# One product in sixteen of a selective scan, on VectorE or on GpSimd

## The chip, the cores and the metric

The kernel runs on one core of a Trainium2 chip. The metric is the device time of one execution in microseconds; each kernel's figure is the median of its timed runs. One further execution is profiled, and its trace gives the durations.

## The reference

Four layers follow each other on an image batch of 4 x 64 x 64 x 128. Layers 0 and 1 are selective state-space scans over the image in four directions (rows, columns, and both backwards), with 128 channels in layer 0 and 256 in layer 1, and 16 states per channel. Layer 2 is a gated message passing over 3 x 3 neighbours, layer 3 a neighbourhood attention. The change lies in the scans of layers 0 and 1. In layer 1's form (layer 0 does the same):

```python
delta = jax.nn.softplus(dts + dt_b[None, :, :, None])
A = -jnp.exp(A_log).reshape(K, DI, N)

def step(h, t):
    x_t, d_t, B_t, C_t = t
    h = jnp.exp(d_t[..., None] * A) * h + (d_t * x_t)[..., None] * B_t[:, :, None, :]
    return (h, jnp.einsum('bkdn,bkn->bkd', h, C_t))
```

For every position, the term that is added to the state is (delta * x) * B, where B belongs to one of 16 states and is the same for all channels; the state times C is summed over the 16 states.

## The kernel before, in words

**Units, steps, tasks.** A task is one image and one block of 128 channels: 4 tasks in layer 0, 8 in layer 1. A task has 16 steps: four directions, each cut into four chunks of 1024 positions (`TS`). There are 192 steps. A step has 16 units (`NG`), numbered here 0 to 15: a unit is 8 channels times 16 states on the 128 partitions, by 1024 positions. Two successive units form a pair, and a pair shares one `h` tile of 128 x 2048.

**The way of a unit.** SP, the queue of SyncE, loads delta * x of 8 channels into the unit's half of the `h` tile, repeated for the 16 states (`load`, line 451), ten units ahead (`LEAD`). TensorE spreads delta into PSUM (`decay`, line 465, tile `da`, two buffers), and ScalarE makes exp(delta * A) of it in place (line 467). VectorE multiplies the pair by B (`times`, line 457), and then runs one `tensor_tensor_scan` for each unit (`scan`, line 476), in place in `h`. ScalarE copies the last states (`save`, line 494), and GpSimd multiplies the pair by C (`times`, line 457 again). TensorE adds up over the states into the bank `yps` (`add_up`, line 557), four units later (`LAG`). After that the `h` tile, one of nine, is free for a new load.

**B and C.** B is repeated over the 8 channels by TensorE into PSUM (`bring_b`, line 502, tile `B`). C is repeated by a transfer: `repeat`, lines 382 to 385, reads each of the 16 rows of C from DRAM eight times into the SBUF tile `repC`, 512 KB.

**Preparation and side work.** For each step, `prepare` computes delta and delta * x 28 units ahead (`AHEAD`), on TensorE, ScalarE and GpSimd (tiles `xd`, `delta`, `low`, `parts`), stores delta * x to DRAM (`dud`), and moves delta's three bf16 parts into place with twelve transfers (line 426). Between the units, a planner sets in "side" work: projections, depthwise convolutions (they load `pad` tiles), convolutions and what comes after the scans, for the images before and behind. Such operations are issued through line 102.

**Order.** The order of every engine is fixed when the program is built; nothing is reordered on the chip. The loop `run` goes over the units and writes scan, products, decay and sums in that order. The class `Plan` keeps an estimated clock, 3.6 us a unit, and an estimated time for TensorE, ScalarE and GpSimd; `slot` adds the cost of a unit's own work, and side work is set in where its estimated start fits. Transfers are posted with a due time and issued by SP in order. Each transfer also waits until the one eight places before it has landed. `fill` adds matmuls with zero weights (line 562) where TensorE has little to do.

Of the kernel before, what the change touches and what calls it, by code (L numbers as in the profile page):

```python
# [10 lines left out]
BF16 = mybir.dt.bfloat16  # L11
# [6 lines left out]
P = 128  # L18
# [3 lines left out]
T = 512  # L22
NCH = L // T
ROWS = T // HW
NS = 16
ND = 4
NG = 16
TS = 1024
# [16 lines left out]
class Consts:  # L45


    def __init__(self, tc, pool, d_gather, d_spread):
        nc = tc.nc

        gather = pool.tile([P, 56], F32, name="gather")
        nc.sync.dma_start(out=gather, in_=d_gather)
        self.gather = [gather[:, 24 - 8 * jj : 56 - 8 * jj] for jj in range(4)]

        self.spread = pool.tile([P, 4, P], BF16, name="spread")
        with tc.tile_pool(name="spread32", bufs=1) as tmp:
            spread = tmp.tile([P, 4, P], F32, name="spread32")
            nc.sync.dma_start(out=spread, in_=d_spread)
            nc.vector.tensor_copy(self.spread, spread)
        self.nothing = pool.tile([P, P], BF16, name="nothing")  # L60
        nc.vector.memset(self.nothing, 0.0)
        self.ones16 = pool.tile([P, T], BF16, name="ones16")
        nc.vector.memset(self.ones16, 1.0)
        self.ident = pool.tile([P, P], F32, name="ident")
        make_identity(nc, self.ident)
        self.ones128 = pool.tile([P, P], F32, name="ones128")
        nc.vector.memset(self.ones128, 1.0 / 128.0)
        self.cen128 = pool.tile([P, P], F32, name="cen128")
        nc.vector.tensor_sub(self.cen128, self.ident, self.ones128)
        self.cen256 = pool.tile([P, P], F32, name="cen256")  # L70
        self.neg256 = pool.tile([P, P], F32, name="neg256")
        nc.vector.memset(self.neg256, -1.0 / 256.0)
        nc.vector.tensor_add(self.cen256, self.ident, self.neg256)
        self.eps = pool.tile([P, 1], F32, name="eps")
        nc.vector.memset(self.eps, EPS)
# [35 lines left out]
UNIT = 3.6  # L111
# [7 lines left out]
class Plan:  # L119
# [22 lines left out]
    def post(self, chain, issue, due=0.0):  # L142

        if self.running:
            self.posted.append((chain, max(self.done, due), issue))
        else:
            issue()
# [11 lines left out]
    def slot(self, u, sums, copies):  # L159
        at = self.at  # L160
        self.now = u * UNIT
        self.flush()
        at["PE"] = max(at["PE"], self.now) + 1.1
        at["ACT"] = max(at["ACT"], at["PE"]) + 1.1
        if u % 2 == 0:
            at["POOL"] = max(at["POOL"], self.now) + 4.5
        at["PE"] += sums
        at["ACT"] += copies

# [111 lines left out]
AHEAD = 28  # L281
LEAD = 10
LAG = 4


class Scans:
# [52 lines left out]
    def prepare(self, t, step):  # L339

        nc, W, half, post = self.plan, t.W, self.half, self.plan.post
        begin = self.plan.now
        k, c = t.steps[step]
        R = W.rank
        rows = R + 2 * NS
        if t.first is None:
            yield "PE" if W.nct > 1 else "PE ACT"

        xd = self.xds[step % 2]
        if t.first is None:  # L350
            xdd = t.xdd[step] = self.dram.tile(
                [rows, TS], F32, name="xdd", tag=f"xdd{W.layer}", bufs=(4, 2 * len(t.steps))[W.layer]
            )
            ps = self.bank()
            for ti in range(W.nct):
                for i in range(HALVES):
                    nc.tensor.matmul(
                        image(ps[i * H : (i + 1) * H, :]),
                        W.xp[:, ti, k, :],
                        self.view(t.xc[ti], k, c, i, HALVES),  # L360
                        start=ti == 0,
                        stop=ti == W.nct - 1,
                    )
                if ti + 1 < W.nct:
                    yield "PE ACT" if ti + 2 == W.nct else "PE"
            nc.scalar.copy(xd, ps)

            def store_xd():
                for i in range(HALVES):
                    nc.sync.dma_start(out=xdd[:, half(i)], in_=xd[i * H : i * H + rows, :])  # L370

            post("prep", store_xd)
            ready = max(self.plan.done, self.plan.now) + LANDING
            yield "PE ACT"
        else:
            xdd, ready = t.first.xdd[step], begin
            for i in range(HALVES):
                nc.sync.dma_start(out=xd[i * H : i * H + rows, :], in_=xdd[:, half(i)])
            yield "PE ACT", self.plan.now + LANDING
        out = t.prepared[step] = {"xd": xd}  # L380

        def repeat():
            out["C"] = self.tile("repC", 2)
            src = bass.AP(xdd.tensor, xdd.offset + (R + NS) * TS, [[TS, NS], [0, 8], [1, TS]])
            nc.sync.dma_start(out=out["C"], in_=src)

        post("rep", repeat, max(begin + 15 * UNIT, ready))

        bias = W.dtb[:, k, t.ct : t.ct + 1]
        delta, low = self.tile("delta", 1), self.tile("low", 1)  # L390
        for i in range(HALVES):
            ps = self.bank()
            nc.tensor.matmul(
                ps,
                W.dtw[i * H : (i + 1) * H, k, t.ct * P : (t.ct + 1) * P],
                xd[i * H : (i + 1) * H, :],
                start=True,
                stop=True,
            )
            nc.scalar.activation(low[:, half(i)], ps, AF.Abs, bias=bias)  # L400
            nc.scalar.activation(delta[:, half(i)], ps, AF.Relu, bias=bias)
            yield "PE ACT" if i + 1 < HALVES else "ACT"
        nc.scalar.activation(low, low, AF.Exp, scale=-1.0)
        yield "ACT"
        nc.scalar.activation(low, low, AF.Ln, bias=1.0)
        yield "POOL"
        nc.gpsimd.tensor_add(delta, delta, low)
        yield "ACT POOL"
        parts = self.tile("parts", 1, shape=(P, 3, TS), dtype=BF16)
        nc.scalar.copy(parts[:, 0, :], delta)  # L410
        nc.gpsimd.tensor_mul(image(low), image(delta), self.view(t.xc[t.ct], k, c, 0, 1))
        yield "POOL"
        t.x_done = step == len(t.steps) - 1
        dud = out["du"] = self.dram.tile([P, TS], F32, name="dud", tag="dud", bufs=3)
        post("prep", lambda: nc.sync.dma_start(out=dud, in_=low))
        nc.gpsimd.tensor_sub(delta, delta, parts[:, 0, :])
        yield "ACT"
        nc.scalar.copy(parts[:, 1, :], delta)
        yield "POOL"
        nc.gpsimd.tensor_sub(parts[:, 2, :], delta, parts[:, 1, :])  # L420


        def own(part, j):
            if j == part == 0:
                out["delta"] = self.dps[step % 2]
            nc.sync.dma_start(
                out=out["delta"][32 * part : 32 * part + 32, j, :], in_=parts[32 * j : 32 * j + 32, part, :]
            )

        for i in range(12):  # L430
            j, part = divmod(i, 3)
            post("rep", lambda part=part, j=j: own(part, j), begin + (11 + 0.5 * i) * UNIT)
        yield ""
# [16 lines left out]
        src = bass.AP(dud.tensor, dud.offset + 8 * g * TS, [[0, NS], [TS, 8], [1, TS]])  # L450
        self.nc.sync.dma_start(out=self.live["h", u // 2][:, u % 2, :], in_=src)

    def times(self, engine, p, name):

        t, step, jj, j, g = self.unit(2 * p)
        pair = self.live["h", p]
        engine.tensor_mul(pair, pair, t.prepared[step][name].unsqueeze(1).to_broadcast([P, 2, TS]))  # L457

    def decay(self, u):
        t, step, jj, j, g = self.unit(u)  # L460
# [98 lines left out]
    def fill(self, cells):  # L559

        for _ in range(min(max(-int((cells - FULL * P * P) // (T * P * P)), 0), 5) if "yps" in self.live else 0):
            self.nc.tensor.matmul(  # L562
                self.live["yps"], self.C.nothing, self.C.ones16, start=False, stop=False, skip_group_check=True
            )

    def keep(self, u):
# [17 lines left out]
    def run(self, between):  # L584

        total = NU * len(self.tasks)
        first = self.tasks[0]
# [7 lines left out]
        for u in range(-12, total + LAG + 1):  # L595
            v = u - LAG
            if 0 <= u < total:
                self.scan(u)
            if u % 2 and -1 <= u < total - 1:
                self.times(self.nc.vector, (u + 1) // 2, "B")  # L600
            if 0 < u <= total and u % 2 == 0:
                self.save(u // 2 - 1)
                self.times(self.nc.gpsimd, u // 2 - 1, "C")
            if 0 <= u + 2 < total:
                self.decay(u + 2)
                if (u + 2) % NG == 0:
# [20 lines left out]
            if rest == 0 and 0 < ahead < total // NG:  # L627
                n, step = divmod(ahead, NU // NG)
# [8 lines left out]
            n, step = divmod(ahead + 1, NU // NG)  # L637
# [5 lines left out]
            if u >= 0:  # L643
                n, i = divmod(u, NU)
# [1564 lines left out]
```

## Time and profile before

| | |
|---|---|
| median of 3 runs | 13472.44 us (13461.69 to 13475.99) |
| the profiled execution | 13484.91 us, its span 13483.1 us |
| mean granted TensorE clock | 0.902 |
| busy in the span: PE, DVE, ACT, POOL | 71%, 87%, 59%, 72% |
| first and last scan of layers 0 and 1 | from 206.9 to 11212.9 us |
| moved by DMA | 2476.31 MB, 184 GB/s on the mean |

Engines: PE is TensorE's matmul, PEld its weight load, DVE VectorE, ACT ScalarE, POOL GpSimd, SP SyncE, which issues the transfers. An instruction group is written as line, engine, operation, output<-inputs, shapes and count, then busy time and the mean of one, then the idle time of its engine just before it and what ended that wait. A wait that ended by several semaphores is put down to the one that came last.

### The profile page before, as it was taken

To read this page: it belongs to the slowest core of one execution; us is meant where nothing else is said; L and a number is where in the kernel's file an instruction comes from. 1 tells how busy PE (TensorE), PEld (TensorE's weight loads), DVE (VectorE), ACT (ScalarE), POOL (GpSimd) and SP (SyncE) were. 2 spreads that over 40 slices of the span, in tenths; PEclk is the share of its full clock that TensorE was granted. 3 is DMA by queue.
4 is the path that set the end of the run, shared out by engine and by line. 5 is a ranking of instruction groups with operands and counts; after the bars stand their busy time and mean duration, and the time that the engine had idled before them with its cause. 6 is when DMAs were issued, how large, how long until landed. Compare 5 with 4: busy or idle time off the path is not lost. (4 is left out here: it accounts for less than half of the span.)

```text
span 13483.1 us, 129941 instructions
## 1 busy us (share of the span) xinstructions
PE 9508.7 (71%) x41730; PEld 2802.6 (21%) x42299; DVE 11700.5 (87%) x6988; ACT 7918.1 (59%) x10594; POOL 9716.6 (72%) x3218
## 2 busy tenths in 40 slices
PE   5776777667667776767766677677777676665788
PEld 1111111111111111111111111122112122111455
DVE  4998999989999889989999999999999992677555
ACT  3666556655665556655665555555555554655577
POOL 3887788878887778778888888888888883345200
PEclk8888999989898889989999899999999988877899
DMA  6888888898888888998889888888888882344200
GB/s 157 215 211 219 222 212 214 223 219 219 198 227 206 208 208 211 221 216 215 204 218 220 219 196 199 200 197 213 202 201 201 197 194 73 84 99 104 65 20 17
DMA packets 877394, 2476.31 MB, mean 184 GB/s; under 512 B 142495, under 2 KB 164135, under 8 KB 868519
## 3 DMA queue, kind: packets, MB, share of 16 engines
q1 hardware_dynamic: 876711, 2467.95, 74.0%
q8 instruction: 337, 5.52, 0.2%
q14 instruction: 346, 2.83, 0.1%
HBM read 2044.11 MB, written 272.37 MB: 172 GB/s over the span
## 5 line engine op out<-in xcount | busy, mean ns | idle before, releaser
L457 POOL TENSOR_TENSOR h<-h,repC 128x2048 f32<-128x2048 f32 x1536 | 6953.0, 4532 | 1536.4 <-ACT state L494 1199.7
L476 DVE TENSOR_TENSOR_SCAN h<-da,state,h 128x1024 f32<-128x1024 f32 x2304 | 5302.8, 2338 | 390.3 <-ACT da L467 270.9
L467 ACT ACTIVATE da<-da,av 128x1024 f32<-128x1024 f32 x3072 | 3338.7, 1088 | 3187.2 <-PE da L465 2847.7
L457 DVE TENSOR_TENSOR h<-h,B 128x2048 f32<-128x2048 f32 x1536 | 3474.6, 2262 | 282.7 <-DMA h<-dud 192.0
L465 PE MATMUL da<-dp,spread 128*128 128x512 bf16 x5753 | 1915.1, 411 | 2253.8 <-DVE h L476 2188.2
L557 PE MATMUL yps<-h,gather 128*32 128x512 f32 x12288 | 1866.2, 683 | 17.6 <-issue 3.8
L476 DVE TENSOR_TENSOR_SCAN h<-da,h 128x1024 f32<-128x1024 f32 x768 | 1722.2, 2279 | 128.0 <-ACT da L467 89.8
L562 PE MATMUL yps<-ones,nothing 128*128 128x512 bf16 x4943 | 1438.4, 403 | 32.9 <-issue 28.1
L465 PEld LDWEIGHTS <-spread 128*128 128x128 bf16 x6144 | 553.0, 101 | 4176.2 <-issue 3656.9
L102 ACT ACT_TABLE_LOAD x600 | 769.8, 1283 | 18.3 <-DMA xcd<-o 5.0
L562 PEld LDWEIGHTS <-nothing 128*128 128x128 bf16 x5121 | 457.0, 101 | 1413.1 <-issue 1092.3
L102 PE MATMUL ms<-d,wts 128*128 128x512 f32 (+3 forms) x900 | 547.5, 717 | 253.8 <-POOL d L102 106.4
L102 POOL TENSOR_TENSOR delta<-delta,low 128x1024 f32<-128x1024 f32 x192 | 451.8, 2353 | 312.2 <-ACT low L102 231.0
L102 ACT CAST parts<-delta 128x1024 bf16<-128x1024 f32 x384 | 400.7, 1044 | 440.4 <-POOL delta L102 415.1
L1919 POOL COPY wide_total<-total 128x128 f32<-128x128 f32 x128 | 37.6, 294 | 831.7 <-DVE total L1917 650.8
L102 PE MATMUL ms<-xd,xpdt 64*128 64x512 f32 x768 | 470.3, 694 | 231.6 <-ACT delta L102 82.4
L540 PE MATMUL yps<-y,ident 128*128 128x512 f32 x576 | 483.9, 928 | 78.2 <-ACT y L574 73.7
L102 POOL TENSOR_TENSOR low<-delta,xc 128x1024 f32<-128x1024 f32 x192 | 503.3, 2622 | 8.9
L1475 ACT ACTIVATE hid<-hid,relb 128x1024 f32<-128x1024 f32 x288 | 322.8, 1146 | 271.2 <-DVE hid L1470 271.0
L1888 ACT ACTIVATE s<-s,least 128x512 f32<-128x512 f32 x512 | 372.2, 727 | 178.9 <-DVE least L1875 178.9
L1875 DVE CUSTOM_DVE_ANT_0 s<-sps,bias 128x512 f32<-128x512 f32 x512 | 323.5, 687 | 173.6 <-PE sps L1864 165.0
L1577 POOL TENSOR_TENSOR acc<-acc,part 128x1024 f32<-128x1024 f32 x120 | 309.4, 2584 | 221.3 <-DVE part L1571 134.5
(291 smaller groups left out, 11191.4 us busy)
## 6 DMA issues: line engine op xcount, KB each, us to landing
h<-dud SPq DMA_DIRECT2D x3072, 512.0 KB
dp<-parts SPq DMA_DIRECT2D x2304, 64.0 KB
repC<-xdd SPq DMA_DIRECT2D x192, 512.0 KB
dud<-low SPq DMA_DIRECT2D x192, 512.0 KB
spread<-gd SPq DMA_DIRECT2D x72, 1024.0 KB
pad<-xid SPq DMA_DIRECT2D x192, 256.0 KB
szd<-o SPq DMA_DIRECT2D x96, 256.0 KB
xcd<-o SPq DMA_DIRECT2D x96, 256.0 KB
```

The costliest lines, as they stand in the source:

```text
L102: return call(*args, **kw)
L457: engine.tensor_mul(pair, pair, t.prepared[step][name].unsqueeze(1).to_broadcast([P, 2, TS]))
L465: self.nc.tensor.matmul(da[:, cols], self.C.spread[:, jj, :], dp[:, j, cols], start=True, stop=True)
L467: self.nc.scalar.activation(da, da, AF.Exp, scale=t.W.a[:, at : at + 1])
L476: nc.vector.tensor_tensor_scan(h[:, way], da[:, way], h[:, way], 0.0 if step % NSTEP == 0 else t.states[step - 1][:, u % NG : u % NG + 1], ...
L540: self.nc.tensor.matmul(self.like_part(yps, k), self.C.ident, self.part(t.y, k, c, b), start=True, stop=False)
L557: self.nc.tensor.matmul(out, self.C.gather[jj], rhs, start=False, stop=jj == 3)
L562: self.nc.tensor.matmul(self.live["yps"], self.C.nothing, self.C.ones16, start=False, stop=False, skip_group_check=True)
L1475: nc.scalar.activation(hid, hid, AF.Gelu, bias=self.relb[:, m, t : t + 1])
L1577: (nc.vector if alone and pair else nc.gpsimd).tensor_add(acc, acc, part)
L1875: self.nc.vector.tensor_tensor_reduce(out=self.live["s", n][:, h, :], in0=self.live["sps", n][:, h, :], in1=self.bias[case][:, h, :], scal ...
L1888: self.nc.scalar.activation(s, s, AF.Exp, scale=-1.0, bias=self.live["least", n][:, h : h + 1], accum_out=self.live["total", n][:, h : h + 1],
```

## The change

In each step, the product by B of unit 7, the second unit of pair 3 (`SHARED`), is done by GpSimd; the other fifteen stay on VectorE. VectorE's product for that pair has 1024 columns in place of 2048. GpSimd's is issued when the scan of unit 4 is, ahead of the product by C of pair 1. It reads B from a new SBUF tile `repB` of 512 KB, with one buffer, which a transfer fills from DRAM as `repC` is filled; the transfer is posted for 20 units after the preparation's start, which is unit 8 of the step before. The planner counts 6.9 instead of 4.5 us for GpSimd in that slot. To make room in SBUF the tile `ones16` goes: the filler matmuls read `spread` in its place, and the scratch memory for dynamic DMA falls from 1024 to 256.

```diff
-        self.ones16 = pool.tile([P, T], BF16, name="ones16")
-        nc.vector.memset(self.ones16, 1.0)
...
-            at["POOL"] = max(at["POOL"], self.now) + 4.5
+            at["POOL"] = max(at["POOL"], self.now) + (6.9 if u % NG == 2 * SHARED - 2 else 4.5)
...
+SHARED = 3
...
-        def repeat():
-            out["C"] = self.tile("repC", 2)
-            src = bass.AP(xdd.tensor, xdd.offset + (R + NS) * TS, [[TS, NS], [0, 8], [1, TS]])
-            nc.sync.dma_start(out=out["C"], in_=src)
+        def repeat(name="C", first=R + NS, bufs=2):
+            out["rep" + name] = self.tile("rep" + name, bufs)
+            src = bass.AP(xdd.tensor, xdd.offset + first * TS, [[TS, NS], [0, 8], [1, TS]])
+            nc.sync.dma_start(out=out["rep" + name], in_=src)
 
         post("rep", repeat, max(begin + 15 * UNIT, ready))
+        post("repB", lambda: repeat("B", R, 1), begin + 20 * UNIT)
...
-    def times(self, engine, p, name):
+    def times_b(self, p):
 
         t, step, jj, j, g = self.unit(2 * p)
+        n = 1 if p % (NG // 2) == SHARED else 2
+        some = self.live["h", p][:, 0:n, :]
+        self.nc.vector.tensor_mul(some, some, t.prepared[step]["B"].unsqueeze(1).to_broadcast([P, n, TS]))
+
+    def times_b_aside(self, p):
+
+        t, step, jj, j, g = self.unit(2 * p)
+        dub = self.live["h", p][:, 1, :]
+        self.nc.gpsimd.tensor_mul(dub, dub, t.prepared[step]["repB"])
+
+    def times_c(self, p):
+
+        t, step, jj, j, g = self.unit(2 * p)
         pair = self.live["h", p]
-        engine.tensor_mul(pair, pair, t.prepared[step][name].unsqueeze(1).to_broadcast([P, 2, TS]))
+        self.nc.gpsimd.tensor_mul(pair, pair, t.prepared[step]["repC"].unsqueeze(1).to_broadcast([P, 2, TS]))
...
-                self.live["yps"], self.C.nothing, self.C.ones16, start=False, stop=False, skip_group_check=True
+                self.live["yps"], self.C.nothing, self.C.spread.rearrange("p j c -> p (j c)"), start=False, stop=False, skip_group_check=True
...
                 self.scan(u)
             if u % 2 and -1 <= u < total - 1:
-                self.times(self.nc.vector, (u + 1) // 2, "B")
+                self.times_b((u + 1) // 2)
+            if 0 <= u < total and u % NG == 2 * SHARED - 2:
+                self.times_b_aside(u // 2 + 1)
             if 0 < u <= total and u % 2 == 0:
                 self.save(u // 2 - 1)
-                self.times(self.nc.gpsimd, u // 2 - 1, "C")
+                self.times_c(u // 2 - 1)
...
-    nc = bacc.Bacc("TRN2", target_bir_lowering=False, num_devices=1, dynamic_dma_scratch_size=1024)
+    nc = bacc.Bacc("TRN2", target_bir_lowering=False, num_devices=1, dynamic_dma_scratch_size=256)
```

## The prediction

> **What bounds the kernel now.** I read the page first, then busy time by windows, the groups with shapes kept apart, the timeline of one step, and the waits last.
>
> The page (name, busy us, share of the span, count):
> ```profile
> span 13483.1 us, 129941 instructions
> PE 9508.7 (71%) x41730; PEld 2802.6 (21%) x42299; DVE 11700.5 (87%) x6988; ACT 7918.1 (59%) x10594; POOL 9716.6 (72%) x3218
> ```
> The share over the whole span mixes the scans with two short layers behind them. The windows view for the scans alone (window, length, then busy us of PE, PEld, DVE, ACT, POOL, granted TensorE clock, DMA share, GB/s):
> ```profile
> 200.00:11220.00 11020.00, 7783.21 (x30881) 2013.12 (x31449) 10392.40 (x4620) 6472.81 (x8006) 9064.17 (x2735) 0.91 0.85 209
> ```
> There DVE is busy 10392 of 11020 us (94%). GpSimd has 9064 us (82%), so some 10 us are free in each of the 192 steps; the DMA engines are at 0.85. The change works here and nowhere else. The groups of the scans, with two of later layers as price rows (mean ns behind the comma):
> ```profile
> L476 DVE TENSOR_TENSOR_SCAN h<-da,state,h 128x1024 f32<-128x1024 f32 x2304 | 5302.8, 2338 | 390.3 <-ACT da L467 270.9 <-DVE h L457 1.8 <-ACT state L494 0.9
> L457 DVE TENSOR_TENSOR h<-h,B 128x2048 f32<-128x2048 f32 x1536 | 3474.6, 2262 | 282.7 <-DMA h<-dud 192.0 <-issue 61.4 <-PE B L502 15.6
> L457 POOL TENSOR_TENSOR h<-h,repC 128x2048 f32<-128x2048 f32 x1536 | 6953.0, 4532 | 1536.4 <-ACT state L494 1199.7 <-DVE h L476 196.9 <-issue 38.0
> L102 POOL TENSOR_TENSOR delta<-delta,low 128x1024 f32<-128x1024 f32 x192 | 451.8, 2353 | 312.2 <-ACT low L102 231.0 <-ACT state L494 51.6 <-DMA h<-dud 17.0
> L1470 DVE TENSOR_TENSOR hid<-cen,near 128x1024 f32<-128x1024 f32 x288 | 336.1, 1211 | 117.6 <-PE cen L1463 117.5
> L1571 DVE TENSOR_TENSOR part<-spread,vals 128x1024 f32<-128x1024 f32 x128 | 235.9, 1859 | 26.4 <-DMA spread<-gd 24.3 <-POOL acc L1577 2.0
> ```
> Two scans and one product by B make a pair. The timeline of a quiet step (start, length, engine, line; bracket: idle before) shows the beat, DVE first, GpSimd below:
> ```profile
> 9105.83 4.59 DVE L476 TENSOR_TENSOR_SCAN h<-da,state,h 128x1024 f32<-128x1024 f32 x2
> 9110.34 2.26 DVE L457 TENSOR_TENSOR h<-h,B 128x2048 f32<-128x2048 f32 x1
> 9112.70 4.59 DVE L476 TENSOR_TENSOR_SCAN h<-da,state,h 128x1024 f32<-128x1024 f32 x2
> ...
> 9106.08 4.51 POOL L457 TENSOR_TENSOR h<-h,repC 128x2048 f32<-128x2048 f32 x1 [0.41 <-ACT state L494]
> 9110.56 1.26 POOL L102 TENSOR_TENSOR o<-o,x 128x512 f32<-128x512 f32 x1
> 9113.62 4.53 POOL L457 TENSOR_TENSOR h<-h,repC 128x2048 f32<-128x2048 f32 x1 [1.80 <-ACT state L494]
> 9119.25 4.52 POOL L457 TENSOR_TENSOR h<-h,repC 128x2048 f32<-128x2048 f32 x1 [1.10 <-ACT state L494]
> ```
> A pair takes 9112.70 - 9105.83 = 6.87 us with DVE never idle, eight pairs 55.0 us. From scan start to scan start, 60 of the 192 steps lie under 55.2 us, the mean is 57.3: most of the stage is DVE's own time, the rest stalls. DVE's gaps of 1 us or more sum to 380 us (123 of them). Of these, 198 us have a PE wait for a DMA beside them, 33 us a wait for GpSimd. The waits (us, times, longest) name the pattern:
> ```profile
> PE ms L102 <- DMA pad<-xid: 136.0, 25, 11.0
> PE ms L102 <- DMA xd<-xdd: 54.1, 13, 10.6
> SPq L451 <- DMA h<-dud: 446.3, 317, 3.7
> ```
> PE works in order; when side work's data land late, the next `da` is late behind it, and so is the scan.
>
> **DVE, taken away.** One product in eight falls from 2048 to 1024 columns. The nearest row with an operand in PSUM is L1470, 1.211 us; halving L457 gives 1.131 as the lower end. Per step 2.262 - 1.211 = 1.05 us, over 192 steps 202 us (217 by halving). The memset of `ones16` runs once: nothing.
>
> **How much DVE can use.** The scans of units 6 and 7 come 1.05 us earlier, but their `da` is made on PE and ACT after the scans of units 4 and 5, which do not move. Over the 192 steps I took the time from the end of the exponential to the start of its scan: 2.75 us in the median for unit 6, 1.65 for unit 7, and under 1.25 in 39% of the steps for unit 7, where PE also has the sums, the next step's projection and the fillers. Capping each step's gain by both margins less 0.1 us leaves 151 of the 202 us. Later waits swallow some of that: in 30% of the steps a scan of units 8 to 15 waits over 1 us, and these hold 41 of the 151 us; I take half, minus 20 (bounds 0 and 83, the gain of the 60% of steps in which some later scan starts the moment ACT ends). Left: 131.
>
> **GpSimd, added.** 192 products of 1024 columns, 2353 ns by the `delta` row (2266 by halving L457): 452 us more on GpSimd, 2.35 in a step with 10 free. It stands ahead of the product by C of units 2 and 3. In the step shown, GpSimd is free from 9111.82 and would do it by 9114.2; the scan of unit 7 starts at 9121.8. The product by C behind it starts 0.6 us late, the next not at all. Over all steps GpSimd idles 5.2 us on the mean ahead of the C products of pairs 1 to 3; in 78% of steps this alone takes in the 2.35, in 91% with pair 4. The following step's preparation on GpSimd begins mostly at units 9 to 13, after that. What waits behind a late product: GpSimd's C products, then PE's sums, then `h` buffers and SP's loads. Cost 0; if the cover is gone, up to the 33 us that sit beside GpSimd now, again.
>
> **The new wait.** In the built program only the scan of unit 7 waits for the new product; the halved DVE product does not. Slack from the end of GpSimd's instruction before the insertion point to that scan: median 7.4 us, least 1.8. It needs 2.35 + 1.05 = 3.4; seven steps fall short, 6 us in total; with 1 us more lag, 29 steps, 23 us. I take 10.
>
> **The transfer, added.** 192 times 512 KB, as `repC`, from SP at unit 8 of the step before, 12 units ahead of use, into one buffer that the earlier step's product has left by unit 7: SP waits for nothing new there. But each transfer on SP also waits for the one eight places ahead (the SPq row), and by units 8 to 12 the DMA share is 0.85 to 0.98 already. In windows of 10 us the engines at 0.95 or more move 250 GB/s, so 0.524 MB is 2.1 us of DMA time. Layer 0 goes from 50.0 busy us in a 58.0 us step to 52.1, layer 1 from 48.1 of 57.0 to 50.2. The `h` loads are issued 10 units ahead and hide it; side loads that PE awaits do not. Lower bound 0: floor steps moved up to 14.5 MB. Upper bound: step length against bytes moved has a slope of 1.57 us per MB, times 0.524 times 192 = 158 us, an overstatement, since steps with more bytes also hold more side work. Below 13 MB the slope is about 0.5; only 38 steps lie above. 0.5 x 0.524 = 0.26 us in 154 steps is 40; 1.3 us, between the whole slope's 0.8 and the 2.1 of DMA time, in 38 steps is 50. Of these 90 I give half to the side work itself: 45.
>
> **Moved.** The planner charges GpSimd 6.9 instead of 4.5 us in one slot, and the built programs differ in the places of side work on PE, ACT, GpSimd and SP; DVE's order is the same. This deals the 123 stalls anew: 0, give or take 35 (their mean of 3.1 us times the square root of 123). Fillers 5121 to 5144, with another moving operand: 23 x 0.4 us on a PE that is 71% busy, nothing; a higher or lower granted clock than 0.91 would change only PE's part of the margins above.
>
> **Against two rules.** GpSimd takes 2353 ns where DVE takes 1211, 1.94 times. The Trainium skill, GPSIMD Engine Reference, 4.1 Engine selection, says to keep elementwise products on VectorE because GpSimd is about twice as slow with two inputs; were GpSimd the path, the sum would be 192 x (2.35 - 1.05) = 250 us slower. The 10 idle us a step speak against that here. The B products on DVE lie between 2253 and 2289 ns beside a GpSimd that is 82% busy, while L1571, with both inputs in SBUF, takes 1859 against 1211. The Trainium skill, SBUF — State Buffer, SBUF: two separate sides, says that a DVE instruction with two SBUF inputs and a GpSimd instruction lock each other out; if that held for these scans, the new 452 us would come on top, but `da` and B lie in PSUM.
>
> **Sum.** 202 - 51 - 20 - 10 - 45 = 76 us off the profiled execution's 13484.9 (span 13483.1). The median of the runs, 13472.4, lies 12.5 lower; the same difference gives 13396.
>
> **The rivals.** (1) Slower: the transfer is the price. If every byte costs the full slope, 158 us go against 121, and the time is 13472 + 37 = 13509. It decides from 0.63 us lost per step (121/192). For it: the saturated windows, and 198 us of stalls beside late DMAs. Against: floor steps at every size. (2) No gain to measure: PE and ACT, not DVE, set the pace once DVE is 1 us early; with 83 swallowed instead of 20 and the rest as above, 13 us remain, 13459. For it: those 60% of steps. Against: the 60 floor steps. (3) Nearly all of it arrives, since every `da` but those of units 6 and 7 follows DVE's earlier scans, and the stalls fall out better: 202 less 10, 13280.
>
> **How the numbers follow.** My forecast 0.56, (1) 0.20, (2) 0.13, (3) 0.11. A measurement can tell about 0.2%, 27 us. The forecast's own range is 13330 (nothing swallowed, the transfer free: 76 + 65 = 141 less) to 13445 (27 less, about a transfer of 90). Faster holds the forecast and (3), same is (2), slower is (1): 0.67, 0.13, 0.20. The range 13280 to 13505 reaches from (3) to (1) and leaves out their outer halves.
>
> **What would show it.** Right: `h<-h,B` at 1024 columns x192 near 1.2 us, DVE about 202 us less, GpSimd 452 more, scans still back to back; the median step near 55 us less 0.8. Wrong: DVE waits at unit 7 for GpSimd; PE's waits for `pad` and `xd` well over 136 and 54 us (rival 1); DVE's waits for ACT up by over 100 us with DMA waits unchanged (rival 2).

## The result and the profile after

The changed kernel took 13561.81 us in the median of 4 runs (13552.99 to 13563.96), beside 13474.22 for the kernel before (4 runs, 13461.69 to 13505.85). The ratio is 1.0059, with a 95% interval from 1.0046 to 1.0073: 87.6 us slower, where 76 us faster was forecast. The profiled execution took 13560.81 us.

The page, its span and the busy time of each engine:
```profile
span 13559.0 us, 130544 instructions
PE 9557.7 (70%) x41751; PEld 2807.3 (21%) x42322; DVE 11510.8 (85%) x6987; ACT 7913.2 (58%) x10594; POOL 10158.8 (75%) x3410
```
DVE lost 190 us of work and the span grew by 76. GpSimd gained 442. The same stretch of the scans in the windows view (same columns as before):
```profile
200.00:11220.00 11020.00, 7783.01 (x30684) 2005.67 (x31251) 10129.24 (x4588) 6442.16 (x7979) 9447.66 (x2914) 0.90 0.89 218
```
The DMA share went from 0.85 to 0.89, and the scans now run past the end of this window. The groups with shapes kept apart:
```profile
L489 DVE TENSOR_TENSOR_SCAN h<-da,state,h 128x1024 f32<-128x1024 f32 x2304 | 5306.9, 2339 | 578.3 <-ACT da L480 450.7 <-POOL h L464 7.0 <-ACT state L507 5.3
...
L464 POOL TENSOR_TENSOR h<-h,repB 128x1024 f32<-128x1024 f32 x192 | 453.9, 2364 | 1.6 <-issue 0.7 <-POOL pad L100 0.3
L458 DVE TENSOR_TENSOR h<-h,B 128x1024 f32<-128x1024 f32 x192 | 229.3, 1194 | 0.0
```
The priced rows are as forecast: the half product takes 1194 ns, GpSimd's 2364, and the scans wait for it 7.0 us in all. What changed is the idle time ahead of the scans, 578.3 us in place of 390.3. A quiet step still has the forecast beat, in the timeline of DVE (the half product at 9060.96), but the median step hardly moved, 55.6 us in place of 55.7:
```profile
9056.46 4.59 DVE L489 TENSOR_TENSOR_SCAN h<-da,state,h 128x1024 f32<-128x1024 f32 x2
9060.96 1.20 DVE L458 TENSOR_TENSOR h<-h,B 128x1024 f32<-128x1024 f32 x1
9062.26 4.59 DVE L489 TENSOR_TENSOR_SCAN h<-da,state,h 128x1024 f32<-128x1024 f32 x2
```
The waits (us, times, longest) say where the time went:
```profile
DVE h L489 <- ACT da L480: 590.2, 304, 19.6
...
PE ms L100 <- DMA pad<-xid: 207.0, 28, 23.3
...
PE ms L100 <- DMA xd<-xdd: 69.6, 23, 9.4
```
DVE waited 360.7 us for `da` before, and PE 136.0 and 54.1 us for these two loads. One such stall, in the timelines of PE and DVE:
```profile
2925.32 1.07 PE L570 MATMUL yps<-h,gather 128*32 128x512 f32 x8
2936.95 1.94 PE L100 MATMUL ms<-pad,diag 128*32 128x512 f32 x8 [10.56 <-DMA pad<-xid]
2938.82 1.03 PE L478 MATMUL da<-dp,spread 128*128 128x512 bf16 x2
...
2929.27 2.35 DVE L489 TENSOR_TENSOR_SCAN h<-da,state,h 128x1024 f32<-128x1024 f32 x1
2941.01 2.35 DVE L489 TENSOR_TENSOR_SCAN h<-da,state,h 128x1024 f32<-128x1024 f32 x1 [9.39 <-ACT da L480]
```
PE stands 10.56 us in front of a convolution whose `pad` has not landed. The `da` of the next unit is queued behind it, and DVE stands idle 9.39 us. DVE's gaps of 1 us or more sum to 626 us in the scans (190 of them; 380 and 123 before). 321 us have a PE wait for a DMA beside them (198 before), 85 a wait for GpSimd (33 before). The steps split by what else runs: tasks 8 to 11, where no convolution loads `pad` tiles, became 0.82 us shorter on the mean (55.06 from 55.88), and tasks 0 to 7 became 1.04 us longer (59.08 from 58.04).

### The profile page after: what moved, and what is told of

It reads as the page before. It is cut to its first block, busy times and chain, and to the rows that moved or that the text cites. A ratio compares the mean times of both kernels' runs of the same rounds, so it can differ in the third digit from the quotient of the medians.

```text
span 13559.0 us, 130544 instructions
## 1 busy us (share of the span) xinstructions
PE 9557.7 (70%) x41751; PEld 2807.3 (21%) x42322; DVE 11510.8 (85%) x6987; ACT 7913.2 (58%) x10594; POOL 10158.8 (75%) x3410
## 5 line engine op out<-in xcount | busy, mean ns | idle before, releaser
L489 DVE TENSOR_TENSOR_SCAN h<-da,state,h 128x1024 f32<-128x1024 f32 x2304 | 5306.9, 2339 | 578.3 <-ACT da L480 450.7
L458 DVE TENSOR_TENSOR h<-h,B 128x2048 f32<-128x2048 f32 (+1 forms) x1536 | 3268.7, 2128 | 308.9 <-DMA h<-dud 208.7
L575 PE MATMUL yps<-spread,nothing 128*128 128x512 bf16 x4962 | 1427.1, 400 | 34.3 <-issue 29.6
L100 PE MATMUL ms<-xd,xpdt 64*128 64x512 f32 x768 | 480.2, 708 | 232.9 <-ACT delta L100 88.1
L100 PE MATMUL ms<-pad,diag 128*32 128x504 f32 (+1 forms) x2304 | 335.4, 683 | 259.4 <-DMA pad<-xid 207.0
```

The lines of the kernel that those rows point to most:

```text
L100: return call(*args, **kw)
L458: self.nc.vector.tensor_mul(some, some, t.prepared[step]["B"].unsqueeze(1).to_broadcast([P, n, TS]))
L489: nc.vector.tensor_tensor_scan(h[:, way], da[:, way], h[:, way], 0.0 if step % NSTEP == 0 else t.states[step - 1][:, u % NG : u % NG + 1], ...
L575: self.nc.tensor.matmul(self.live["yps"], self.C.nothing, self.C.spread.rearrange("p j c -> p (j c)"), start=False, stop=False, skip_group ...
```

## The experiments

Four causes were open: the transfer, GpSimd's load, relief that never reaches the end, and the planner's new order. The charge in `slot` alone decides that order; a new order, with its own places for the side work, is called a new deal below. Every kernel with charge 4.5 below has on PE, ACT, GpSimd and SP the order of the kernel before, apart from the rows that it adds, and every kernel with 6.9 the order of the changed one. So the parts can be compared one by one. Each diff is against the changed kernel. Differences are between medians, each against the kernel before as it was measured beside that run (13477.31 to 13482.33), and by the intervals each is good to some 12 to 26 us; a difference of two such differences is less sure still. The ratio is an estimate of its own and can lie up to 0.0007 (9 us) from that of the two medians. The stage is the time from the start of the first scan to the end of the last.

### The edits around it

`none`: charge 4.5, all products on DVE, no transfer. What stays are the filler's operand and the smaller scratch memory.
```diff
-            at["POOL"] = max(at["POOL"], self.now) + (6.9 if u % NG == 2 * SHARED - 2 else 4.5)
+            at["POOL"] = max(at["POOL"], self.now) + 4.5
...
-        post("repB", lambda: repeat("B", R, 1), begin + 20 * UNIT)
...
-        n = 1 if p % (NG // 2) == SHARED else 2
+        n = 2
...
-            if 0 <= u < total and u % NG == 2 * SHARED - 2:
-                self.times_b_aside(u // 2 + 1)
```


> Only the change's side edits: the fillers read spread in place of the ones, the dynamic scratch memory is 256; no transfer, no product on GpSimd, the old charge. If the parts measured so far (+66 for the transfer, -40 for the product, +47 for the order, each with these side edits) are each their own, this one is within 15 us of before. If the side edits cost something themselves, it is 15 to 30 us slower, and each part is smaller by that.

13474.98 us, 2.3 less than before, ratio 0.9995 (0.9986 to 1.0005). These edits cost nothing, and `none` is the base for the traces below.

### DVE's relief alone

`d_only`: as `none`, with `n` kept at 1, so that unit 7's product is on no engine.

> VectorE's relief alone: the product of unit 7 is left out altogether (its B is missing), nothing is added on GpSimd or SP, old order. Theory H (VectorE's saved time is handed back by TensorE and ScalarE in units 6 to 15, whoever does the product): like the product on GpSimd alone, 25 to 60 us faster than before, 13415 to 13450. Theory P (the 452 us added on GpSimd eat the gain): 110 to 160 us faster than before, 13315 to 13365.

13383.16 us, 94.2 less, ratio 0.993 (0.9911 to 0.9949). The waits of `none`, then of `d_only`:
```profile
DVE h L488 <- ACT da L479: 380.2, 229, 12.0
...
PE ms L100 <- DMA pad<-xid: 121.5, 22, 11.0
...
PE ms L100 <- DMA xd<-xdd: 65.8, 17, 10.4
```
```profile
DVE h L488 <- ACT da L479: 478.3, 300, 13.2
...
PE ms L100 <- DMA pad<-xid: 118.4, 22, 10.3
...
PE ms L100 <- DMA xd<-xdd: 82.3, 20, 15.7
```
Nothing was added, and DVE waits 98 us longer for `da`. PE's wait for `pad` from `xid` did not grow; that for `xd` did, by 16.5 us. DVE's busy time in the scans fell by 196 us; its gaps grew by 105: by 42 ahead of the scans of units 6 and 7, by 45 ahead of those of units 8 to 15, by 18 elsewhere. 196 - 105 = 91 us is what the stage became shorter. About half of the relief is all that arrives in this order.

### GpSimd's product

`g_only`: the product is on GpSimd, charge 4.5, no transfer; it reads `repC`, which is there.
```diff
-        self.nc.gpsimd.tensor_mul(dub, dub, t.prepared[step]["repB"])
+        self.nc.gpsimd.tensor_mul(dub, dub, t.prepared[step]["repC"])
```


> Of the change only the product on GpSimd is kept: it reads the tile of C in place of B's (a wrong factor, the same shape and place), so that no transfer is added; the planner charges 4.5 us, the order is that of before. Theory T: most of the predicted gain arrives, 80 to 150 us faster than before, 13320 to 13395. Theory G: slower than before by 50 us or more. Theory N (DVE's time is handed back as waits for PE and ACT whatever is done): within 27 us of before.

13438.57 us, 39.8 less, ratio 0.9967 (0.9956 to 0.9978). Against `d_only` GpSimd's work costs 54 us, though only 30 between the two profiled spans (13419.0 and 13389.5), so its size is less sure than its sign. The stalls with a wait for GpSimd beside them go from 29 us in `none` to 69. Between the traces of `d_only` and `g_only` the stage grew by 28 us: DVE was busy 12 us longer and idle 16 us longer.

`p_only`: all products stay on DVE, and GpSimd does a product that nobody reads.
```diff
-        dub = self.live["h", p][:, 1, :]
-        self.nc.gpsimd.tensor_mul(dub, dub, t.prepared[step]["repB"])
+        rep = t.prepared[step]["repC"]
+        self.nc.gpsimd.tensor_mul(self.tile("repB", 1), rep, rep)
```


> GpSimd's load alone: VectorE keeps all sixteen products; in the place of the new product GpSimd multiplies the tile of C by itself into the unused tile repB, 128x1024, which nobody reads. Theory H: within 20 us of before. Theory P: 60 to 120 us slower than before.

13506.98 us, 29.7 more, ratio 1.0017 (1.0008 to 1.0027). The dose was smaller than meant, as the group shows:
```profile
L463 POOL TENSOR_TENSOR repB<-repC 128x1024 f32<-128x1024 f32 x192 | 363.9, 1895 | 0.6
```
364 us in place of 454. GpSimd had some 10 free us in a step, its product takes 1.9, no scan waits for it, and the kernel is slower all the same. The load is not free. Of the 28 us by which the stage is longer than in `none`, 18 are busy time of DVE and 10 idle time. Of the 18, 15 lie in one small instruction, `skip`, which the last section shows. The price has no one place: against `d_only`, `g_only` lost 26 of its 28 us in tasks 8 to 11, against `none`, `p_only` lost 21 of its 28 in tasks 0 to 7.

### The transfer

`t_only`: as `none`, with the transfer, which nobody reads.

> Of the change only the transfer of B into SBUF (192 times 512 KB) is kept; nothing reads it, all sixteen products stay on VectorE, and the planner charges 4.5 us as before, so that every other instruction stands where it stood. Theory T (the transfer makes side loads late, and TensorE waits for them in order): 70 to 160 us slower than before, 13540 to 13630, and DVE's gaps of 1 us and more grow from 380 us by about as much. Theory G (the product on GpSimd is what costs) and theory C (the planner's new order): within 27 us of before.

13544.94 us, 66.6 more, ratio 1.005 (1.0035 to 1.0065). Its window of the scans and its waits:
```profile
200.00:11220.00 11020.00, 7854.76 (x31295) 2005.74 (x31295) 10335.72 (x4599) 6455.65 (x7992) 9027.84 (x2727) 0.91 0.89 218
```
```profile
DVE h L489 <- ACT da L480: 414.0, 228, 15.2
...
PE ms L100 <- DMA pad<-xid: 155.4, 30, 11.5
...
PE ms L100 <- DMA pad<-ld: 75.0, 7, 18.3
PE ms L100 <- DMA xd<-xdd: 71.9, 14, 14.5
```
The DMA share goes from 0.85 to 0.89, PE's wait for `pad` from `xid` from 121.5 to 155.4 us, that for `pad` from `ld` from 52.7 to 75.0, and the stalls beside a DMA from 218 to 252. Counted more narrowly, as DVE gaps of 1 us or more that overlap a wait of PE of 1 us or more for a DMA, they go from 145 to 199. Between these two traces the stage grew by 48 us and the span by 47, less than the 69 between the medians. In the changed kernel the transfer is issued 12 units ahead of its use, and GpSimd idles 1.6 us in all ahead of the products that read it (the row with `repB` above); what is late is the other loads. The steps say so too. The transfer runs in every step, but `pad` tiles are loaded in tasks 0 to 7 alone, and there the stage became 60 us longer, while tasks 8 to 11 became 12 us shorter. The split does not separate `pad` from other side work of those tasks. Part of the lateness is that SP issues the loads later: the 264 loads of `pad` from `xid` were issued 1.6 us later on the mean in `t_only` than in `none` (14.8 after 13.2 us, each counted from the scan twelve units before the `h` load that SP had issued last).

`tg`: transfer and product, charge 4.5: the whole change but for the order.

> The whole change, but for the planner's charge, which stays 4.5 us: transfer and product with the old order. Theory C: 40 to 130 us faster than before. Theory T: the sum of the transfer alone and the product alone, between 20 us faster and 60 us slower than before. Theory G: like the changed kernel, 13560.

13510.2 us, 31.8 more, ratio 1.0023 (1.0013 to 1.0032). The transfer adds 72 us to `g_only` (88 between the profiled spans), much as it adds 69 to `none`, and again in tasks 0 to 7 alone (93 us longer, tasks 8 to 11 11 us shorter). Both causes add up.

`g_act`: the product on GpSimd, and B copied out of PSUM by ScalarE in place of the transfer.
```diff
-            at["POOL"] = max(at["POOL"], self.now) + (6.9 if u % NG == 2 * SHARED - 2 else 4.5)
+            at["POOL"] = max(at["POOL"], self.now) + 4.5
...
-        post("repB", lambda: repeat("B", R, 1), begin + 20 * UNIT)
...
+            if u >= 0 and u % NG == 1:
+                now = self.tasks[u // NU].prepared[u % NU // NG]
+                now["repB"] = self.tile("repB", 1)
+                self.nc.scalar.copy(now["repB"], now["B"])
```


> A version of the change without the transfer: the product on GpSimd, its B copied from PSUM to SBUF by ScalarE (192 copies of 128x1024 at unit 1, some 1.05 us each by the cast row), old charge and order. If the transfer's cost is DMA time, this lies near the product alone with C's tile: 13420 to 13460, faster than before by 20 to 60 us. If ScalarE's 200 us fall on the path, it is 20 us or more slower than before.

13447.82 us, 29.5 less, ratio 0.9971 (0.996 to 0.9982): 61 us less than `tg`, and 10 more than `g_only`, which is within the noise. The copy, on an engine that is 59% busy:
```profile
L625 ACT COPY repB<-B 128x1024 f32<-128x1024 f32 x192 | 195.1, 1016 | 26.5 <-DVE h L457 25.6
```

### The planner's order

`c_only`: as `none`, with the charge of 6.9 kept. No work is added or removed but a few fillers.

> Only the planner's charge of 6.9 us in one GpSimd slot per step, and so the new order of side work, is kept; the products and transfers are those of before. Theory C (the new order deals the stalls worse): 60 to 150 us slower than before, with DVE's gaps larger by as much. Theories T and G: within 35 us of before, the spread I gave a new deal.

13525.67 us, 47.3 more, ratio 1.0037 (1.0025 to 1.005).

`c_52` and `c_80`: the same with other charges.
```diff
-            at["POOL"] = max(at["POOL"], self.now) + (6.9 if u % NG == 2 * SHARED - 2 else 4.5)
+            at["POOL"] = max(at["POOL"], self.now) + (5.2 if u % NG == 2 * SHARED - 2 else 4.5)
```


> Planner's charge alone again, 5.2 us in place of 6.9, with the products and transfers of before. If the 47 us of the charge of 6.9 are one unlucky deal of side work, another charge falls anywhere within 50 us of before, either side. If charging GpSimd more is bad in itself, the cost grows with the charge: 10 to 20 us slower here.

13447.0 us, 34.5 less, ratio 0.9972 (0.996 to 0.9984).

> Planner's charge alone, 8.0 us. An unlucky deal: anywhere within 50 us of before. A cost that grows with the charge: 55 to 90 us slower than before.

13450.26 us, 31.2 less, ratio 0.9979 (0.9969 to 0.9988). With 4.5, 5.2, 6.9 and 8.0 the time moves by 0, -34.5, +47.3 and -31.2 us: there is no trend in the charge, each value is another deal. Against `c_only`, on its own order, the changed kernel shows its parts: DVE's busy time in the stage 10199.4 in place of 10388.7 us, its gaps of 1 us or more 626 in place of 414, of which those beside a DMA 321 in place of 193. Its tasks 0 to 7 are 79 us longer, its tasks 8 to 11 38 us shorter.

`land_after` and `land_before`: the changed kernel, and `none`, with later planned places for side work that awaits a transfer.
```diff
-LANDING = 10.0
-FOUR_LANDING = 14.0
-ROWS_LANDING = 18.0
+LANDING = 13.0
+FOUR_LANDING = 17.0
+ROWS_LANDING = 22.0
```


> The changed kernel with the planner told that transfers land later: 13, 17 and 22 us in place of 10, 14 and 18. It does the same work with the same transfers. Theory T says that the transfer costs because TensorE reaches side work whose loads have not landed: this kernel then waits less for pad and xd (207 and 70 us in the changed kernel) and is 40 to 120 us faster than it, 13440 to 13520. If the DMA engines themselves are the bound, it stays within 30 us of 13562.

13515.92 us, 34.4 more than before, ratio 1.0028 (1.0018 to 1.0038), 53 less than the changed kernel's 87.6. The sign that was expected with it is missing: PE's wait for `pad` from `xid` is 216.0 us after 207.0; those for `xd` and for `pad` from `ld` fell, from 69.6 to 41.6 and from 55.0 to 34.1.

> The control: the same later landings in the kernel of before (with the side edits that cost nothing). Theory T: it also waits less for pad and xd (136 and 54 us before), 20 to 80 us faster than before, 13395 to 13455, less than the changed kernel gains from it.

13467.99 us, 13.5 less, ratio 0.9986 (0.9977 to 0.9995). More time for landing helps the kernel with the transfer more (53 against 11 us). But here too the wait for `pad` from `xid` grew, from 121.5 to 151.5 us. The edit deals the order anew, and the deals above differ by as much, so this pair settles nothing.

### The parts on other orders

`t_80`, `all_80` and `all_52`: the transfer alone, and the whole change, in the orders of the charges 8.0 and 5.2.

> The transfer alone, on the order of the charge 8.0 (which alone gave 13450). If the transfer's 66 us are its own: 40 to 90 us slower than that, 13490 to 13540. If they belonged to the first order: within 25 us of 13450.

13535.03 us, 52.7 more, ratio 1.0042 (1.0027 to 1.0057): 84 above `c_80`. By the traces tasks 0 to 7 are 94 us longer than in `c_80`, tasks 8 to 11 7.

> The whole change with a charge of 8.0 in place of 6.9. By the parts, -31 for this order, +66 for the transfer, -40 for the product: 13475, within 35 us of before. If the change itself is what costs, whatever the order: 13530 or more.

13491.1 us, 8.8 more, ratio 1.0009 (1.0 to 1.0019): 40 above `c_80`.

> The whole change with a charge of 5.2. By the parts, -34, +66 and -40: 13470, within 35 us of before. If the change itself is what costs, whatever the order: 13530 or more.

13461.65 us, 20.7 less, ratio 0.9987 (0.9977 to 0.9996): 14 above `c_52`. Against its own order the whole change costs 34, 14, 40 and 40 us with the charges 4.5, 5.2, 6.9 and 8.0; the 14 alone are within the noise. That it is slower than the kernel before by 88 us is half the deal; that it does not pay on any of four orders is the change.

`g_act_52`: `g_act` in the order of 5.2.

> The version with ScalarE's copy in place of the transfer, with a charge of 5.2. By the parts (-30 for the version, -34 for the order): 13415, 60 us faster than before. If orders and parts do not add: anywhere from 13400 to 13480.

13394.24 us, 88.1 less, ratio 0.9937 (0.9922 to 0.9952). It beats both kernels. Some 34 us of it is the order (`c_52`), 54 the product on GpSimd with B copied by ScalarE; against `all_52`, 67 us come from dropping the transfer. Its window and waits:
```profile
200.00:11220.00 11020.00, 7906.60 (x31528) 2018.89 (x31528) 10202.08 (x4620) 6677.70 (x8257) 9529.33 (x2948) 0.91 0.85 210
```
```profile
DVE h L488 <- ACT da L479: 455.4, 288, 19.3
...
PE ms L100 <- DMA pad<-xid: 159.9, 30, 11.3
```
DVE is relieved as in the changed kernel and the DMA share is back at 0.85; PE waits 159.9 us for `pad` from `xid`, in place of 203.9 in `all_52`, which has the same order. DVE's wait for `da` still stands 105 us above that of `c_52` (350.5).

## Why the prediction was wrong

Adding the parts in turn gives a chain of medians, each against the kernel before: `none` -2.3, `d_only` -94.2, `g_only` -39.8, `tg` +31.8, the changed kernel +87.6. Its steps stand beside the prediction's terms:

| step | forecast | measured |
|---|---|---|
| edits around it | 0 | -2 |
| DVE's relief that arrives (202 - 51 - 20) | -131 | -92 |
| GpSimd's product and the new wait | 0 + 10 | +54 |
| the transfer | +45 | +72 |
| the planner's order | 0 | +56 |
| sum | -76 | +88 |

**DVE, taken away: right.** 1211 ns was taken, 1194 measured; 202 us forecast, 196 less busy in `d_only`.

**How much DVE can use: the part for units 8 to 15 was mis-sized.** Units 6 and 7 lost 42 us where 51 was forecast. "Later waits swallow some of that ... I take half, minus 20 (bounds 0 and 83)": they took 45, within the bounds. The likely reason, which no run isolates: the count of scans that already waited over 1 us cannot see a scan that waits for nothing only because DVE itself is late; the upper bound, made from the 60% of steps in which a scan starts the moment ACT ends, does see it. Another 18 us lie where no loss was forecast.

**GpSimd, added: "Cost 0; if the cover is gone, up to the 33 us" failed.** Room on the mean (5.2 us idle ahead of three C products) is not room in each step. That idle time fell to 3.3 us in the changed kernel, and the first C product behind the new one began on the mean 7.01 us after the end of the pair's second scan in place of 5.19: 1.8 us late, where the step that the prediction showed gave 0.6. The C products feed PE's sums, which free `h`. The prediction followed only this path. A part of the price lies elsewhere, in DVE's own `skip`: 15 of the 28 us by which the stage of `p_only` is longer than that of `none`. The price of 54 (30 by the profiled spans, 32 in `p_only` against `none`) lies above the bound of 33 or near it. The new wait was 7.0 us where 10 was forecast. The Trainium skill, GPSIMD Engine Reference, 4.1 Engine selection, puts elementwise products on VectorE because GpSimd is about twice as slow with two inputs. The rows agree on the speed (2364 against 1194 ns). Were GpSimd the path, the prediction's sum for that case is 250 us slower; the runs put product and relief together at 38 us faster (`g_only` against `none`). So most of GpSimd's 454 us, though not all, went into its idle time.

**The transfer: right mechanism, too small.** 45 was taken of bounds 0 and 158; 72, 69 and 84 were measured. The side loads that PE awaits come late, as written, and the price lies in the tasks that load `pad`. Giving half of the 90 to the side work itself was the error; the full 90 would have been near. Rival 1 had the sign and its mark, the longer waits for `pad`, but not its mechanism alone: the transfer stayed under the 121 us from which it was to decide. Rival 2's mark was DVE's waits for ACT up by over 100 us with DMA waits unchanged. `d_only` comes near it, with 98 us, of which some may belong to the longer wait for `xd` (16.5): that mechanism acts too.

**Moved: "0, give or take 35" was the largest miss** (56 us; 50 by `c_only` against `none`). The orders came out at -34.5, +47.3 and -31.2 us against the old one, which fits a deal of some 40 us. So the width was fair and the draw bad luck, but the prediction's range left it out: every case in it had this term at its mean. Each of the other misses also went the same way, and 39 + 44 + 27 + 56 us, less 2, are the 164 between forecast and result.

What stays open is the way from GpSimd's load to the end, beyond what `skip` takes: the neighbours of the stalls name it, but the price differs between medians and spans and between the two pairs of runs. For the transfer, no run separates loads that SP issues later from loads that land later once issued. Nor do the runs say which property makes one order better than another.

## What to carry to other kernels

Busy time taken from the busiest engine is worth only what the next-latest producer lets through, here 92 of 196 us, and leaving the work out altogether measures that ceiling in one run. Before moving work, price each thing that it is moved to by the stalls that others suffer there: a transfer with twelve units of slack cost 69 to 84 us, because it made other loads late, and a copy on an engine with room cost 10 (`g_act` against `g_only`), no more than the noise. Where an edit also touches a planner's cost, run the cost alone and the change under several costs; otherwise a deal of 40 us passes for the effect.

## What the runs showed of the hardware

**A small DVE instruction waits out GpSimd.** `skip` (128x128, operands in SBUF, once a task) takes 277 to 281 ns alone. In `p_only` it took up to 8.24 us, in the timelines of DVE and GpSimd:
```profile
8581.19 8.24 DVE L542 TENSOR_SCALAR skip<-ident,dsum 128x128 f32<-128x128 f32 x1
8589.35 4.46 DVE L488 TENSOR_TENSOR_SCAN h<-da,h 128x1024 f32<-128x1024 f32 x2
...
8579.16 4.51 POOL L469 TENSOR_TENSOR h<-h,repC 128x2048 f32<-128x2048 f32 x1
8583.63 1.26 POOL L100 TENSOR_TENSOR d<-d,big 128x512 f32<-128x512 f32 x1
8584.85 4.49 POOL L469 TENSOR_TENSOR h<-h,repC 128x2048 f32<-128x2048 f32 x1
```
GpSimd has three instructions in a row, and DVE's ends 0.09 us after the third. Every lengthened `skip` in the traces of six kernels ends some 0.1 us after an instruction of GpSimd. Its twelve sum to 16.0 us in `none`, 30.7 in `p_only`, 18.3 in `d_only` and 29.8 in `g_only`: 12 to 15 us more DVE time with GpSimd's load. That depends on what GpSimd does at twelve moments: in `t_only`, with the load of `none`, the sum is 9.4. The scans and the products by B, with an operand in PSUM, kept their 2339 and 2261 ns. The Trainium skill, SBUF — State Buffer, Who interferes with whom, describes such an exclusion: `tensor_scalar` can enter a mode that uses both of VectorE's port pairs, and then it or GpSimd, whichever issues second, waits for the other's whole instruction; outside these modes an instruction with at most one input in SBUF does not contend. The rows here fit that, but none shows in which mode `skip` ran, and it waited for three instructions and not one. The prediction weighed the exclusion for the scans alone.

**A product of a tile by itself is quicker on GpSimd:** 1895 ns (`repC` times `repC`, into a third tile) against 2364 for two tiles of the same size. In the kernel before, the 32 squares `sqs<-norm` of 128x512 take 1041 ns in the median, the products `norm<-norm,rstd` 1270.

**Busier DMA engines did not slow the packets.** Packets of 4 KB took 266 ns on the mean in `none` and in `t_only`; the windows of 10 us in which the engines are 0.95 busy or more went from some 490 to some 590 of 1102. That points to loads waiting in line, in part before SP issues them; the traces hold no time from issue to landing that would show the rest.

**The granted clock in the scans** fell from 0.914 to 0.902. It was 0.911 with the transfer alone, 0.909 with the product alone and 0.917 in `none`; what lowers it was not settled. It does not decide the time by itself: `all_52` had 0.903 and was 21 us faster than the kernel before.
